# Transposing graph masks by DMA instead of on TensorE, and computing symmetric attention scores from their upper blocks only

## The chip, the cores and the metric

The kernel runs on one core of a Trainium2 chip. The metric is the device time of one execution in microseconds (us). A core has a matrix engine (TensorE; PE in the profile, with its weight loads as PEld), VectorE (DVE), ScalarE (ACT), GpSimd (POOL) and SyncE (SP), which here only issues DMA transfers. All work in parallel, each through its own instructions in order, and wait for each other by semaphores.

## The reference

Thirty-two graphs of 512 nodes with 256 features pass through four layers. Every layer normalises `x`, applies a ReLU, runs a graph layer and adds the result to `x`. The masks come from `adj`, which has an entry for each pair of nodes.

```
for each graph (x is 512 x 256, adj is 512 x 512, integers):
  layer 0: 4 heads; e = leaky_relu(src_i + dst_j), masked by adj > 0, softmax over j, times Wh, ELU
  layer 1: e = leaky_relu(s1_i + s2_j), masked by adj > 0, softmax over i, times h W, ELU
  layer 2: e = leaky_relu( sum_d h[i,d] a_k[d] h[j,d] ), a_k picked by adj == k+1
           alpha = softmax over j; out = alpha h
  layer 3: transformer block of 8 heads, mask adj | adj^T | eye, feed-forward 256 -> 1024 -> 256, two layer norms
  x = x + layer(relu(layernorm(x)))       (no change of shape between layers)
```

In the inputs `adj` holds only 0 and 1 and is symmetric with a full diagonal. In layer 2 then only `a_0` is used, and the raw score `e` is symmetric in i and j by its formula, whatever the inputs.

## The kernel before

**What a graph's work is.** A graph's rows are cut into `NT = 4` tiles of 128. `masks` makes `m = max(adj, 0)` in bf16 (tag `e0`), its transpose `mT` (tag `mT`, three buffers) and `m3`, the union of both with the diagonal, for layer 3. It transposes by TensorE: for each block column j, four 128x128 transposes with `ident_b` into one PSUM tile `ps_m`, then a VectorE copy into `mT[:, j]`. `layer0` to `layer3` follow. Most matmuls have f32 operands, and each of those appears in the profile as two passes with a weight load each; transposes of f32 data (`ps_t`) take one.

**Layer 0 around the masks.** The factors of the softmax are worked out per row (`rt`), transposed (`ps_sp`), copied (`spr`), written to DRAM (`rows0_d`) and read back spread over all partitions (`rows0`, 1 MB). Each of 16 products `p0` is one VectorE operation on `rows0`, `rt` and `mT[:, j]`. So the first `p0` needs `rows0` and a `mT`. The products feed the matmuls into `ps_o`.

**Layer 2 before.** With `h2T` the transposed features and `ha` the same scaled by `a_0`, each block row j of the scores is one PSUM tile `ps_e` of 128x512, from two f32 matmuls over the two halves of the features. ScalarE takes two exponentials of it (`y1`, `y2`), VectorE their maximum and its product with `mT[:, j]`, which is `p[:, j]`. Then `ps_o2` takes four matmuls for each row tile, over the four `p[:, j]`.

**What sets the order.** Nothing is emitted directly. Every operation is recorded as a job of a `Plan`, on one engine, in the order of the code. A table of whole numbers, `PLACES`, gives each job of a graph its place; graph b's jobs lie `b * ROUND` later, and places of one graph span about five `ROUND`s, so that up to five or six graphs are in work at once. `carry_out` sorts all jobs by place and chains those of each engine in that order:

```python
j.place = (self.number * ROUND + self.table[self.at], self.at)
```

The costs that the code gives beside each operation (as the `0.7` of `plan.matmuls(0.7, ...)`) are the planner's and have no effect when the kernel is built. All DMAs of the graphs are issued by SP in this one order (`plan.dma`, line 229). All DVE, ACT and POOL operations carry the helper's line 208 in the profile, matmuls 242 and transposes 240.

`Kind` gives buffers in turn. PSUM tags `ps_a` and `ps_b` have two slots each; `ps_m`, `ps_t`, `ps_e`, `ps_sp` and others all take turns in `ps_a`.

Of the kernel before, what the change touches and what calls it, by code (L numbers as in the profile page):

```python
# [12 lines left out]
BF = mybir.dt.bfloat16  # L13
I32 = mybir.dt.int32
U8 = mybir.dt.uint8
AF = mybir.ActivationFunctionType
# [3 lines left out]
P = 128  # L20
EPS = 1e-5
SLOPE = 0.2
# [100 lines left out]
class Plan:  # L123
# [5 lines left out]
        tensor_mul=(1, 2), tensor_add=(1, 2), tensor_max=(1, 2), scalar_tensor_tensor=(1, 3),  # L129
# [120 lines left out]
def cut(i, n):  # L250
    return slice(i * n, (i + 1) * n)
# [6 lines left out]
def width(args):  # L258
# [4 lines left out]

ROUND = 100000
PLACES = [
    101057, 0, 123766, 132584, 138431, 138431, 129046, 129834, 141740, 143105, 134508, 134509, 144040, 210061,
    161002, 171169, 182168, 133665, 13191, 13021, 30954, 43154, 22726, 43431, 38536, 68458, 82755, 86554,
    111786, 130752, 129745, 131659, 123328, 131022, 131022, 131659, 131659, 132269, 131903, 131903, 133024,
    133024, 133652, 134925, 134925, 135696, 134926, 135221, 136062, 136062, 136599, 136118, 136118, 137150,
    137150, 137545, 137150, 137150, 139783, 140391, 142870, 141719, 141719, 143128, 143129, 144853, 148260,  # L270
    148260, 152426, 148876, 155076, 157818, 157819, 157819, 157819, 164437, 164708, 163596, 155574, 152987,
    160713, 176876, 177710, 177710, 179541, 182264, 183463, 176075, 182822, 185309, 181512, 188918, 191812,
    194790, 194790, 195416, 200809, 186592, 166060, 200276, 196368, 206502, 219397, 219397, 220179, 220236,
    220236, 220993, 220993, 220993, 236727, 260248, 225731, 224396, 221012, 226847, 227931, 225205, 226679,
    229220, 229909, 230823, 231592, 233629, 234505, 234416, 235736, 236254, 236255, 236255, 236658, 236658,
    235736, 235736, 235736, 235737, 235737, 238980, 239538, 240610, 238111, 238111, 238138, 238912, 238912,
    239366, 238681, 238681, 238759, 245139, 243744, 247134, 245207, 246602, 251006, 252746, 255282, 256553,
    256553, 267976, 284322, 258231, 258231, 266098, 274931, 278417, 259592, 268181, 276573, 276814, 280405,
    258871, 269299, 271252, 271252, 276979, 286007, 286230, 286230, 286719, 286775, 284782, 285553, 285553,
    285554, 286042, 304459, 316500, 292215, 286775, 286775, 286712, 286042, 286947, 286999, 286712, 286042,  # L280
    289012, 290864, 292270, 295476, 295301, 295110, 300417, 301246, 301273, 301546, 301877, 303799, 304417,
    304978, 304978, 304978, 305067, 305193, 305509, 305551, 305551, 307045, 307452, 312018, 312812, 308660,
    308660, 308661, 309600, 309600, 318033, 314173, 314173, 314937, 314173, 314937, 319853, 320002, 320002,
    320288, 320059, 320288, 320288, 322248, 322248, 322403, 323086, 324116, 324117, 325432, 326217, 328750,
    326427, 329903, 331583, 335374, 344646, 332413, 334123, 331714, 333807, 334483, 334355, 336218, 333807,
    336218, 342666, 350313, 355600, 351966, 356396, 352228, 358089, 358678, 360971, 360971, 360971, 360971,
    363748, 363748, 364342, 369127, 379803, 380423, 380423, 382964, 384060, 384225, 371529, 374051, 378404,
    379308, 383266, 381312, 383855, 383855, 383855, 384091, 384645, 384645, 384645, 384645, 385299, 385400,
    385400, 385400, 385400, 389820, 388261, 386697, 387002, 387597, 387826, 400724, 398878, 392051, 393887,
    394199, 394199, 404354, 403089, 401043, 401043, 404073, 405950, 407212, 407456, 407456, 407584, 413067,  # L290
    415663, 415663, 420500, 420500, 420500, 405416, 406883, 405416, 406883, 409976, 409216, 407761, 407761,
    407761, 407761, 418999, 418111, 412219, 414095, 414095, 414095, 421851, 420227, 418886, 419104, 419104,
    419859, 422460, 421229, 422921, 429525, 422921, 422921, 422921, 428527, 429230, 429525, 356784, 429933,
    430027, 431151, 431151, 433611, 433611, 435044, 435044, 435798, 415663, 455098, 467528, 430623, 437997,
    437034, 435798, 436926, 438396, 438153, 438202, 438170, 438463, 438463, 439032, 439044, 439854, 439997,
    440219, 439866, 439866, 440054, 440689, 440689, 440689, 440690, 440690, 443133, 443701, 454267, 467213,
    448784, 448785, 448785, 448785, 448785, 450704, 444131, 444131, 445620, 445620, 445620, 445620, 445901,
    446700, 446700, 446700, 446701, 446701, 449901, 449901, 449901, 450807, 460195, 461219, 459629, 463106,
    463106, 463106, 463106, 463106, 463106, 463207, 464695, 464695, 464695, 464695, 464695, 464696, 464696,
    465450, 467213, 465756, 465756, 465756, 465756, 466107, 466107, 466108, 466561, 466561, 467895, 467931,  # L300
    467931, 467932, 467932, 467932, 467932, 471404, 467213, 468235, 473585, 474076, 467537, 472797, 474594,
    474655, 475293, 475293, 475293, 478979, 479362, 479362, 479362, 479362, 480230, 503393,
]


# [1 line left out]
def quick_path(  # L307
# [6 lines left out]
    B, N, D = x.shape  # L314
    NT = N // P
    KD = D // P
# [31 lines left out]
    def new(tag, name, shape, dtype=F32):  # L348
        return plan.tile(K[tag], name, shape, dtype)
# [133 lines left out]
    def masks(b, adj_t):  # L483


        m = new("e0", f"m_{b}", [P, NT, N], BF)
        plan.dve("tensor_scalar_max", m, adj_t, 0, each=0.52e-3)
        kinds = new("kinds", "kinds", [P, 1])
        plan.act("activation", adj_t, adj_t, AF.Relu, bias=none, accum_out=kinds, fixed=0.5)
        mT = new("mT", f"mT_{b}", [P, NT, N], BF)  # L490
        for j in range(NT):
            ps = new("ps_a", "ps_m", [P, NT, P], BF)
            plan.matmuls(0.7, *((ps[:, i], m[:, i, cut(j, P)], ident_b) for i in range(NT)))
            plan.dve("tensor_copy", mT[:, j], ps.shaped("p a b -> p (a b)"), each=0.52e-3)
        m3 = new("m3", f"m3_{b}", [P, NT, N], BF)
        plan.dve("tensor_max", m3, m, mT, each=0.52e-3)
        for i in range(NT):
            plan.dve("tensor_max", m3[:, i, cut(i, P)], m3[:, i, cut(i, P)], ident_b, each=0.52e-3)
        plan.dve("scalar_tensor_tensor", ok[:, 0:1], kinds, 0.0, ok[:, 0:1], OP.is_le, OP.mult)
        return mT, m3  # L500
# [100 lines left out]
    def layer2(b, x_t, mT):  # L601
        h = new("h1", f"h2_{b}", [P, NT, D + 1])
        plan.pool("memset", h[:, :, D], 1.0)
        normed(x_t, h, AF.Relu)
        hT = transposed_a(h, "h1T", f"h2T_{b}")
        ha = new("wh1", f"ha_{b}", [P, NT, D + 2])
        ha_k = [ha[:, 2 * k : 2 * k + 2, :D] for k in range(KD)]
        for k in range(KD):
            plan.dve(
                "tensor_scalar_mul", ha_k[k], hT[:, k].split("p (a b) -> p a b", (2, D), a=2), a2_t[:, k : k + 1],  # L610
                each=0.52e-3, fixed=0.2,
            )
        p = new("p1", f"p2_{b}", [P, NT, N])
        for j in range(NT):
            ps = new("ps_a", "ps_e", [P, N])
            for k in range(KD):
                plan.matmuls(FULL, (ps, ha_k[k][:, j // 2, cut(j % 2, P)], hT[:, k], k == 0, k == KD - 1))

            y1, y2 = (new("y", "y2", [P, N]) for _ in range(2))
            plan.act("activation", y1, ps, AF.Exp, bias=nshift, fixed=0.27)  # L620
            plan.act("activation", y2, ps, AF.Exp, bias=nshift, scale=SLOPE, fixed=0.27)
            plan.dve("tensor_max", y1, y1, y2)
            plan.dve("tensor_mul", p[:, j], y1, mT[:, j])
        inv = new("inv2", "inv2", [P, NT])
        for i in range(NT):
            ps = new("ps_a", "ps_o2", [P, N])
            plan.matmuls(
                NT * HALF,
                *((ps[:, : D + 1], p[:, j, cut(i, P)], h[:, j], j == 0, j == NT - 1) for j in range(NT)),
            )  # L630
            plan.dve("reciprocal", inv[:, i : i + 1], ps[:, D : D + 1], fixed=0.16)
            plan.dve(
                "scalar_tensor_tensor", x_t[:, i], ps[:, :D], inv[:, i : i + 1], x_t[:, i], OP.mult, OP.add, fixed=0.21
            )
        within(inv, NT)
# [630 lines left out]
```

## Time and profile before

| | |
|---|---|
| median of 10 runs | 3957.23 us (3953.45 to 3960.96) |
| profiled execution | 3958.52 us, span of the profile 3956.7 us |
| mean granted TensorE clock | 0.979 |
| PE busy | 3785.6 us, 96% of the span |
| PE weight loads | 2383.9 us, 60% |
| DVE busy | 2596.2 us, 66% |
| ACT busy | 1891.2 us, 48% |
| POOL busy | 781.0 us, 20% |
| from one graph's output transfer to the next, in the middle | 117.9 us |

"Busy" is the time in which at least one instruction of the engine is in work. Matmuls overlap: one with 512 columns is shown as 592 ns, but the next of its kind starts 429 ns after it. In a group of instructions the mean is that of one, and the idle time is that of the engine just before the instructions of the group. The window view gives the busy time of each engine in a stretch of the span.

### The profile page before, as it was taken

The page shows a single profiled execution, that of the slowest core. Times are in us where ns is not written, and L with a number is a line of the kernel's source. Part 1 is how long each engine was busy: PE and PEld are TensorE (multiplying, and loading weights), DVE is VectorE, ACT ScalarE, POOL GpSimd, SP SyncE. Part 2 cuts the span into 40 slices and gives each one's busy share as a digit, 9 for nine tenths or more (in the row PEclk, how much of TensorE's full clock was granted, in tenths as well). Part 3 has the DMA queues.
Part 4 walks back from the last instruction along what each step waited for, and adds up shares of the span by engine and source line. Part 5 has one row for each costly group of instructions (what it writes and reads, how often), then busy time and mean ns, then how long its engine had stood idle before and what let it go on. Part 6 is the DMA issues. An engine that isn't in the chain of part 4 may idle for free. (4 is left out here: it accounts for less than half of the span.)

```text
span 3956.7 us, 51981 instructions
## 1 busy us (share of the span) xinstructions
PE 3785.6 (96%) x20294; PEld 2383.9 (60%) x20294; DVE 2596.2 (66%) x5115; ACT 1891.2 (48%) x3297; POOL 781.0 (20%) x618
## 2 busy tenths in 40 slices
PE   5799999999999999999999999999999999999996
PEld 4556666656666556566656666656666655666543
DVE  4576666767666776666776666776766676766532
ACT  1255444555444554444555544555444455544442
POOL 0011222111222112222121222211122211222211
PEclk7799999999999999999999999999999999999998
DMA  3111110110110110110110110111111011110000
GB/s 99 48 34 33 38 44 23 44 44 28 41 41 23 44 44 28 41 41 23 44 44 28 42 40 28 38 44 34 37 38 43 24 44 40 32 34 27 17 12 13
DMA packets 99278, 144.62 MB, mean 37 GB/s; under 512 B 29008, under 2 KB 65360, under 8 KB 94928
## 3 DMA queue, kind: packets, MB, share of 16 engines
q1 hardware_dynamic: 92672, 136.22, 10.8%
q10 hardware_dynamic: 6352, 4.99, 0.4%
q8 instruction: 162, 2.65, 0.3%
q14 instruction: 92, 0.75, 0.1%
HBM read 122.96 MB, written 18.22 MB: 36 GB/s over the span
## 5 line engine op out<-in xcount | busy, mean ns | idle before, releaser
L242 PEld LDWEIGHTS ps_o<-wh,p 128*128 128x128 f32 x5120 | 706.8, 197 | 252.1 <-issue 183.8
L208 DVE TENSOR_TENSOR p<-p,m 128x2048 f32<-128x2048 f32 x256 | 582.3, 2285 | 332.0 <-ACT p L208 327.6
L242 PE MATMUL ps_o<-wh,p 128*128 128x65 f32 (+1 forms) x5120 | 762.1, 303 | 27.9 <-DVE p L208 27.9
L208 ACT ACTIVATE p<-ps_s 128x1024 f32<-128x1024 f32 x512 | 496.5, 1021 | 331.1 <-PE ps_s L242 255.8
L208 POOL TENSOR_SCALAR rstd<-mv 128x4 f32<-128x4 f32 x192 | 105.4, 549 | 2493.9 <-DVE mv L208 2201.6
L208 DVE SCALAR_TENSOR_TENSOR p<-rows,rt,mT 128x512 f32<-128x512 f32 x512 | 431.6, 865 | 250.1 <-PE ps_o L242 140.2
L242 PE MATMUL ps_f<-tT,ff_t 128*128 128x512 f32 x1024 | 455.8, 600 | 13.7 <-ACT tT L208 13.7
L242 PE MATMUL ps_f<-ff_t,f 128*128 128x256 f32 x2048 | 457.6, 379 | 0.0
L242 PEld LDWEIGHTS ps_f<-ff_t,f 128*128 128x128 f32 x2048 | 381.9, 190 | 48.5 <-issue 0.5
L208 ACT ACTIVATE h<-x,shift,rstd 128x256 f32<-128x256 f32 x512 | 275.1, 593 | 208.3 <-DVE shift L208 123.4
L242 PEld LDWEIGHTS ps_f<-tT,ff_t 128*128 128x128 f32 x1024 | 191.2, 192 | 248.7 <-issue 212.9
L242 PE MATMUL ps_s<-qk 32*128 32x512 f32 x2048 | 297.2, 642 | 0.3
L242 PE MATMUL ps_to<-p,ones 128*32 128x512 f32 x2048 | 267.8, 606 | 10.0 <-DVE p L208 10.0
L208 ACT ACTIVATE f<-ps_f,ff1b_c 128x512 f32<-128x512 f32 x256 | 161.3, 681 | 240.2 <-PE ps_f L242 240.2
L242 PE MATMUL ps_ct<-p,v 128*32 128x512 f32 x2048 | 272.2, 604 | 0.4 <-DVE p L208 0.4
L242 PE MATMUL ps_e<-h2T,ha 128*128 128x512 f32 x512 | 253.9, 618 | 2.5 <-ACT y L208 1.9
L242 PE MATMUL ps_o<-h,p 128*128 128x257 f32 x1024 | 239.7, 386 | 1.9 <-DVE mv L208 1.1
L242 PE MATMUL ps_qk<-h3T,wqkv_t 128*128 128x512 f32 x512 | 239.8, 602 | 1.1 <-ACT h3T L208 1.1
L242 PEld LDWEIGHTS ps_o<-h,p 128*128 128x128 f32 x1024 | 188.7, 189 | 79.7 <-issue 54.5
L208 DVE TENSOR_TENSOR u<-ps_f,n 128x512 f32<-128x512 f32 x64 | 44.3, 692 | 276.1 <-PE ps_f L242 276.1
L208 DVE BATCH_NORM_STATS2 st<-x 128x6 f32<-128x256 f32 x512 | 205.6, 414 | 8.2 <-DMA x<-in_x_dram 4.9
L208 POOL TENSOR_TENSOR rstd<-rstd,nhalf 128x4 f32<-128x4 f32 x192 | 208.3, 1089 | 13.4
(114 smaller groups left out, 4838.4 us busy)
## 6 DMA issues: line engine op xcount, KB each, us to landing
adj<-in_adj_dram SPq DMA_DIRECT2D x32, 1024.0 KB
rows<-rows_d SPq DMA_DIRECT2D x32, 1024.0 KB
x<-in_x_dram SPq DMA_DIRECT2D x32, 512.0 KB
rows<-rows_d SPq DMA_DIRECT2D x32, 512.0 KB
inv<-in_d SPq DMA_DIRECT2D x256, 64.0 KB
out_dram<-y SPq DMA_DIRECT2D x32, 512.0 KB
ff_t<-in_L_gnn_W_dram ACTq DMA_DIRECT2D x2, 1024.0 KB
to_d<-to SPq DMA_DIRECT2D x64, 8.0 KB
```

The costliest lines, as they stand in the source:

```text
L208: return [getattr(unit, method)(*map(real, args), **{k: real(v) for k, v in kw.items()})]
L242: made.append(self.nc.tensor.matmul(*map(real, c[:3]), start=c[3], stop=c[4]))
```

## The change

The masks are no longer transposed by TensorE. For each row tile i of `m` SP issues one DMA transpose, which moves the 128x512 bf16 tile into column block i of all four `mT[:, j]`. Every `mT[:, j]` is complete only when all four have landed.

In layer 2, of block row j only the column blocks from j on are worked out: `ps_e` has 512, 384, 256 and 128 columns, and so have the exponentials and the maximum. The blocks below the diagonal are had by transposing the blocks `y1[:, i]` with i > j on TensorE into a new PSUM tile `ps_y` (six 128x128 f32 transposes for each graph), and VectorE multiplies `ps_y` with the mask into `p`. `PLACES` is a new table as a whole, so that every engine's order changes.

```diff
 PLACES = [
-    101057, 0, 123766, 132584, 138431, 138431, 129046, 129834, 141740, 143105, 134508, 134509, 144040, 210061,
...
+    5095, 0, 75421, 87257, 75421, 75422, 79730, 91873, 132389, 236254, 196081, 207636, 243857, 181976, 44107,
...
         mT = new("mT", f"mT_{b}", [P, NT, N], BF)
-        for j in range(NT):
-            ps = new("ps_a", "ps_m", [P, NT, P], BF)
-            plan.matmuls(0.7, *((ps[:, i], m[:, i, cut(j, P)], ident_b) for i in range(NT)))
-            plan.dve("tensor_copy", mT[:, j], ps.shaped("p a b -> p (a b)"), each=0.52e-3)
+        for i in range(NT):
+            plan.dma(mT[:, :, cut(i, P)], m[:, i], 0.5, 1.2, "dma_start_transpose")
...
         p = new("p1", f"p2_{b}", [P, NT, N])
         for j in range(NT):
+            on = slice(j * P, N)
             ps = new("ps_a", "ps_e", [P, N])
             for k in range(KD):
-                plan.matmuls(FULL, (ps, ha_k[k][:, j // 2, cut(j % 2, P)], hT[:, k], k == 0, k == KD - 1))
+                plan.matmuls(
+                    FULL * (NT - j) / NT,
+                    (ps[:, on], ha_k[k][:, j // 2, cut(j % 2, P)], hT[:, k, on], k == 0, k == KD - 1),
+                )
 
             y1, y2 = (new("y", "y2", [P, N]) for _ in range(2))
-            plan.act("activation", y1, ps, AF.Exp, bias=nshift, fixed=0.27)
-            plan.act("activation", y2, ps, AF.Exp, bias=nshift, scale=SLOPE, fixed=0.27)
-            plan.dve("tensor_max", y1, y1, y2)
-            plan.dve("tensor_mul", p[:, j], y1, mT[:, j])
+            plan.act("activation", y1[:, on], ps[:, on], AF.Exp, bias=nshift, fixed=0.27)
+            plan.act("activation", y2[:, on], ps[:, on], AF.Exp, bias=nshift, scale=SLOPE, fixed=0.27)
+            plan.dve("tensor_max", y1[:, on], y1[:, on], y2[:, on])
+            if j < NT - 1:
+                ps = new("ps_a", "ps_y", [P, NT, P])
+                for i in range(j + 1, NT):
+                    plan.matmuls(0.11, (ps[:, i], y1[:, cut(i, P)], ident))
+                plan.dve("tensor_mul", p[:, j + 1 :, cut(j, P)], ps[:, j + 1 :], mT[:, j + 1 :, cut(j, P)])
+            plan.dve("tensor_mul", p[:, j, on], y1[:, on], mT[:, j, on])
```

In the order of SP, the first three transposes of a graph stand after the read of the layer 1 rows (`rows1`) of the graph two before. The fourth stands between the write of the same graph's `rows0_d` and the read of `rows0`, and the loads of the next graph follow.

## The prediction

> **What bounds the kernel now.** The first view is the page's table of 40 slices, the second the window view.
>
> ```profile
> PE   5799999999999999999999999999999999999996
> DVE  4576666767666776666776666776766676766532
> PEclk7799999999999999999999999999999999999998
> ```
>
> ```profile
> 0.00:200.00 200.00, 126.05 (x556) 103.44 (x557) 102.72 (x252) 46.48 (x105) 13.56 (x26) 0.74 0.23 73
> 200.00:3800.00 3600.00, 3543.72 (x19278) 2219.79 (x19277) 2459.10 (x4797) 1799.20 (x3126) 737.82 (x572) 1.00 0.11 36
> 3800.00:3956.00 156.00, 115.84 (x464) 60.63 (x462) 34.43 (x68) 45.54 (x66) 29.64 (x20) 0.84 0.04 11
> ```
>
> The columns after the length are PE, PEld, DVE, ACT and POOL busy, then granted clock, DMA share and GB/s. From 200 to 3800 us PE is busy 98.4% of the time at the full clock; DVE stands at 68%, ACT at 50%, the DMA engines at 11%. At 117.9 us between outputs this stretch is 30.5 of the 32 graphs, and only 56 us of it, 1.8 us for each graph, have no matmul. So PE's work sets the time, and what leaves PE comes off the time unless a new wait replaces it. The third view is the groups by form:
>
> ```profile
> L242 PE MATMUL ps_f<-ff_t,f 128*128 128x256 f32 x2048 | 457.6, 379 | 0.0
> L242 PE MATMUL ps_f<-tT,ff_t 128*128 128x512 f32 x1024 | 455.8, 600 | 13.7 <-ACT tT L208 13.7
> L242 PE MATMUL ps_e<-h2T,ha 128*128 128x512 f32 x512 | 253.9, 618 | 2.5 <-ACT y L208 1.9 <-DVE ha L208 0.5
> L240 PE MATMUL ps_t<-ident,h 128*128 128x128 f32 x1024 | 173.4, 284 | 13.4 <-ACT h L208 12.0 <-DVE mT L208 0.7 <-DVE inv L208 0.6
> L240 PE MATMUL ps_m<-ident_b,m 128*128 128x128 bf16 x512 | 50.2, 221 | 9.9 <-DVE m L208 6.1 <-DVE h0T L208 1.1 <-DVE bo_r L410 0.5
> ```
>
> Since matmuls overlap, the price of one is not its mean but busy time over count: 0.445 us for a pass of 512 columns (455.8/1024), 0.223 for 256 (457.6/2048), 0.169 for a 128x128 f32 transpose (173.4/1024, ends of short groups included).
>
> **The change, part by part, all 32 graphs together.**
>
> *Mask transposes leave PE.* The `ps_m` group is 50.2 us busy and 9.9 idle: a gain of 50 to 60 us; I take 55.
>
> *Fewer score columns.* Each graph had 16 passes of 512. It will have four each of 512, 384, 256 and 128. At 0.445, 0.334 (between its neighbours), 0.223 and 0.14 (between half of 0.223 and 0.169) that is 4 x 1.142 = 4.57 us against 16 x 0.445 = 7.12, a gain of 2.55 us for each graph, 82 us in all. Taking 6/16 off the group's own 253.9 us gives 95. I take 85, since the passes of `ps_e` stand in pairs and their ends are in the group's figure.
>
> *Six f32 transposes for each graph come to PE.* 192 x 0.169 = 32 us, which I take; 192 x 0.11 = 21 if they follow each other closely, 192 x 0.284 = 55 if each stands alone. The built order has them as three and three single ones.
>
> PE in sum: -55 - 85 + 32 = -108 us, bounds -78 (50 + 82 - 54) and -134 (60 + 95 - 21). In 91% of the span (3600 of 3957 us) PE is full; in the rest chains and loads bound it, and I count half: -108 x 0.955 = -103.
>
> *The other engines get lighter.* DVE loses 128 mask copies (53.1 us) and 6/16 of the columns of the maximum and of the product (87.4 and 85.4 us busy; less than 6/16 off, since a short operation has a fixed part). It gains three products from PSUM of 384, 256 and 128 columns; near rows are 0.42 us for 256 (`o<-ps_o,rt`) and 0.69 for 512, so about 1.25 us for each graph. Net near -2 us of 81 a graph. ACT drops by about 1.5 us a graph. Neither is the bound, so both count nothing by themselves.
>
> *The transposes on SP.* This is the unknown: the trace shows no DMA transpose. What it shows is SP's normal work and how soon the rows come back:
>
> ```profile
> 2058.53 0.30 SPq L229 DMA_DIRECT2D rows_d<-spr  x1
> 2059.86 0.34 SPq L229 DMA_DIRECT2D rows<-rows_d  x1
> ...
> 2064.80 1.41 DVE L208 SCALAR_TENSOR_TENSOR p<-rows,rt,mT 128x512 f32<-128x512 f32 x2 [3.45 <-DMA rows<-rows_d]
> ```
>
> An issue takes SP 0.3 us; `rows0_d` has landed 1.33 us after its issue began, and `p0` starts 4.8 us (here 4.9) after the read's issue. Say that each transpose holds SP, and the transfers behind it, for x us. The lowest x is 0.3, the row above. A high one: 128x512 bf16 values in runs of one 128-row column (256 bytes) are 512 packets; the page's q1 row has 92672 packets in 10.8% of 16 engines' 3957 us, 74 ns each, so 512 x 74 / 16 = 2.4 us. Packets of single elements would be far worse, 128 times that, and nothing in the trace excludes them. I take 1.4, in the middle of 0.3 and 2.4, because the transfer has plain whole rows at its source like the ordinary ones.
>
> What covers x? In the built order, between `m` and the fourth transpose PE has 32 passes of `ps_o` in layer 1 at 0.215 (6.9 us), 16 of `ps_wh` at 0.223 (3.6), two of `ps_qk` and four of `ps_v` (1.7), and three `ps_s`, two `ps_to` and two `ps_ct` groups at about 0.95 (6.7): 18.9 us. From `spr` to the first `p0` stand two `ps_s`, two `ps_to` and two `ps_ct` groups (5.8), eight `ps_t` (0.9) and `ps_e` of 512 and 384 columns (3.0): 9.7 us. `m` itself takes 1.2 us. So rows0's read is issued the later of 1.33 and 0.3 + x us after `rows0_d`'s issue, and the `p0` is due at 18.9 + 9.7 = 28.6 us after `m` begins. For x over 1.0 it can start at max(18.9, 1.2 + 3x) + 0.3 + x + 4.8. At x = 1.4 that is 25.4: 3.2 us early. Nothing is late for x up to 4.6 us. Queued behind a transpose on SP are only rows0's write and read, then the next graph's `x` and `adj` (used half a round later) and an output, which nobody waits for. The waits for `to_d`, `part`, `in_d` and `inv` come over 10 us of matmuls later. So I cost SP's part at nothing.
>
> Here a rule of the skill speaks against the change. The Trainium skill, "VectorE: DVE Perf Modes", section "The three transpose paths", gives 390 ns for a 128x128 bf16 transpose on TensorE and 1309 ns for one by DMA, and advises TensorE where PSUM will do. The `ps_m` row shows 98 ns each on TensorE (50.2/512), so the page's TensorE price is not this kernel's. By the page's DMA price, an estimate, x would be 4 x 1.309 = 5.2 us, and `p0` 0.6 us late: some 19 us of the gain gone, not all.
>
> *The new chain in layer 2.* `ps_e` to two exponentials (0.68 each), maximum (0.68 or less), `ps_y`, product, `ps_o2`. It needs 2.1 us and hops before `ps_y`. The built order has 5 to 6 us of other matmuls between each `ps_e` and its transposes (`ps_s`, `ps_ct`, `ps_to` groups), so it is covered; PSUM loses four holders of `ps_a` a graph and gains three. I cost it at nothing; without the cover it is 2 us for each of three block rows.
>
> *Waits on PE that may go.* Of PE's idle time 27.9 us are waits of `ps_o` for a DVE `p`, in the same stage where DVE now waits 3.4 us a graph for `rows0` (the waits view, 109.8 us in all). The new order puts 9.7 us between `spr` and `p0`, so this DVE wait should go. I count a third of the 27.9, -10, between 0 and -28, and +15 for unknown new waits on the other side.
>
> The profiled execution took 3958.5 us, 1.8 more than its span and 1.3 more than the median. 3958.5 - 103 - 10 - 1.3 = 3844 us. The forecast's own range is 3805 to 3890: the PE bounds, with waits from -20 to +15.
>
> **Rivals.**
>
> *Slow transposes: slower than before.* If x is above 4.6 us, `p0` comes late, DVE stands with the layer 3 products `p3` queued behind it, and soon PE waits for `ps_to` and `ps_ct`. By the formula it is even with before where the delay equals the 3.4 us a graph that PE gains, at x = 6.4. At x = 8 `p0` starts at 25.2 + 13.1 = 38.3, 9.7 late: 6.3 net a graph, times 31 is 195, so 4152 us. For it: no row prices a DMA transpose. Against: the DMA engines are only 11% busy, and 256-byte packets give 2.4. A delay at `p0` is here taken as fully PE's.
>
> *The gain is partly given back.* The table is new as a whole, so other waits of PE can open, above all in layer 2: half of its 6 us cover missing would cost 1 us for each of three block rows, 3 x 31 = 93 us, and leave 3937, at worst no change. For it: `ps_y` sits on a chain over three engines. Against: the distances in the built order.
>
> *The work isn't saved.* Symmetric scores need the lower blocks too; if the order still had 16 full passes nothing would be gained. The built order shows the short ones, so this has no chance of its own.
>
> **How the numbers follow.** My forecast has 0.72, the given-back gain 0.13 (3890 to 3948), slow transposes 0.12, and 0.03 is left for no change. A measurement can tell 0.2% of this kernel, 8 us. Faster: 0.72 + 0.13 = 0.85; same 0.03; slower 0.12. The range takes in my own and the greater part of the second case: 3790 to 3935.
>
> **What would show it.** Right: outputs 114 to 115 us apart; no `ps_m` group; 512 `ps_e` passes with together 150 to 170 us busy; 192 `ps_y`; SP's transposes each 0.3 to 2.4 us, with the fourth of a graph delaying `rows` by under 2 us; no long DVE wait for `rows`. Wrong: transposes over 4.6 us, DVE waiting for `mT` or `rows` with PE idle before `ps_o` or `ps_to`; or PE idle before `ps_y` or `ps_o` of layer 2 for more than 1 us a graph.

## The result, and the profile after

The change made the kernel slower: 3976.24 us (median, 3970.73 to 3982.79) against 3956.47, a ratio of 1.005 with an interval of 1.0041 to 1.0059. The forecast was 3844 us, range 3790 to 3935. The profiled execution has a span of 3968.4 us and a mean granted clock of 0.978.

The window view of after, with the columns of before:

```profile
0.00:200.00 200.00, 125.61 (x551) 104.38 (x552) 96.84 (x239) 41.30 (x99) 8.53 (x23) 0.76 0.28 83
200.00:3800.00 3600.00, 3503.62 (x18926) 2174.67 (x18926) 2413.22 (x4766) 1740.79 (x3132) 733.23 (x575) 1.00 0.14 40
3800.00:3968.00 168.00, 121.85 (x501) 65.84 (x499) 40.96 (x78) 45.94 (x67) 29.75 (x20) 0.84 0.05 14
```

In the middle TensorE is busy 3503.6 of 3600 us, where it was 3543.7. So work did leave it, and the idle time grew from 56 to 96 us. Outputs follow each other by 118 us on average, as before. The groups by form show that the planned work is there:

```profile
L242 PE MATMUL ps_e<-h2T,ha 128*128 128x512 f32 x128 | 63.4, 618 | 1.0 <-DVE m L208 1.0
L242 PE MATMUL ps_e<-h2T,ha 128*128 128x384 f32 x128 | 58.0, 536 | 0.0
L240 PE MATMUL ps_y<-ident,y 128*128 128x128 f32 x192 | 49.0, 310 | 0.8 <-DVE y L208 0.8
L242 PE MATMUL ps_e<-h2T,ha 128*128 128x256 f32 x128 | 36.2, 405 | 1.6 <-DVE p L208 1.6
L242 PE MATMUL ps_e<-h2T,ha 128*128 128x128 f32 x128 | 19.6, 276 | 0.0
```

The `ps_e` passes are busy 177.2 us in sum where they were 253.9 (the prediction's sign of being right was 150 to 170), `ps_m` is gone, and `ps_y` waits for nothing (0.8 us in all). The transposes on SP are as cheap as assumed. This line of the view of the tile `mT` has least, median and longest time in ns:

```profile
L229 SPq DMA_TRANSPOSE mT<-m x128: 1188/1251/2372, 16.7 to 3553.3; - x128
```

What TensorE waits for shows the difference. The waits view, first of before and then of after, each over 20 periods from 1000 us on (total, number, longest):

```profile
PE ps_wh L242 <- ACT rt L208: 10.0, 20, 0.5
PE ps_f L242 <- ACT tT L208: 7.7, 20, 0.4
PE ps_wo L242 <- DVE cT L208: 5.6, 19, 0.4
PE ps_t L240 <- ACT h L208: 4.6, 20, 0.2
PE ps_sp L240 <- ACT rt L208: 3.5, 20, 0.2
```

```profile
PE ps_f L242 <- DVE o L208: 25.0, 20, 1.3
PE ps_t L240 <- ACT h L208: 21.8, 60, 0.8
PE ps_wo L242 <- DVE cT L208: 5.4, 5, 1.4
PE ps_t L240 <- DVE h1T L208: 2.0, 3, 0.8
```

Most of the old small waits are gone, and two new ones take their place: 1.25 us a graph for VectorE's `o` and 1.1 us for ScalarE's `h`. Neither is in layer 2 or at the masks. The timeline of after shows where the second comes from (start, length, engine):

```profile
2108.43 2.35 POOL L208 TENSOR_TENSOR x<-x,b_r 128x1024 f32<-128x1024 f32 x1
2108.49 2.30 DVE L208 SCALAR_TENSOR_TENSOR shift<-mv,rstd 128x4 f32<-128x4 f32 x1 [1.47 <-POOL rstd L208]
...
2110.83 0.60 ACT L208 ACTIVATE y<-u,shift,rstd 128x256 f32<-128x256 f32 x1 [2.19 <-DVE shift L208]
...
2111.34 2.06 ACT L208 ACTIVATE h<-x,shift,rstd 128x256 f32<-128x256 f32 x4
...
2111.98 0.82 PE L240 MATMUL ps_t<-ident,h 128*128 128x128 f32 x3 [0.76 <-ACT h L208]
```

`shift` is 4 columns wide and takes 2.30 us. It begins 0.06 us after a GpSimd operation of 1024 columns and ends with it; ScalarE's `y` and `h` and TensorE's `ps_t` stand behind it. The wait for `o` begins in the same way, 36 us earlier:

```profile
2072.47 2.35 POOL L208 TENSOR_TENSOR n<-n,g_r 128x1024 f32<-128x1024 f32 x1
2072.53 2.31 DVE L208 SCALAR_TENSOR_TENSOR shift<-mv,rstd 128x4 f32<-128x4 f32 x1 [1.47 <-POOL rstd L208]
...
2074.76 3.45 DVE L208 TENSOR_TENSOR mc<-rows,mT 128x512 f32<-128x512 f32 x2
...
2074.89 2.76 POOL L208 TENSOR_TENSOR n<-n,b_r 128x1024 f32<-128x1024 f32 x1
...
2079.72 0.42 DVE L208 TENSOR_TENSOR o<-ps_o,rt 128x256 f32<-128x256 f32 x1
...
2080.28 1.10 PE L242 MATMUL ps_f<-ff_t,f 128*128 128x256 f32 x4 [1.25 <-DVE o L208]
```

Here a blocked `shift` and then a blocked `mc` hold up VectorE's queue, in which `o` stands five operations later. The view of the tile `shift`, first of before, then of after:

```profile
L208 DVE SCALAR_TENSOR_TENSOR shift<-mv,rstd x192: 139/161/165, 15.1 to 3944.7; 128x4 f32<-128x4 f32 x192
```

```profile
L208 DVE SCALAR_TENSOR_TENSOR shift<-mv,rstd x192: 148/161/2312, 15.3 to 3956.4; 128x4 f32<-128x4 f32 x192
```

Of after's 192 `shift` 61 take over 1 us, of before's none. All 61 begin inside a GpSimd operation of 1024 columns, 32 times `x` and 29 times `n`. The Trainium skill, "SBUF — State Buffer", section "SBUF: two separate sides", says that VectorE and GpSimd share one pair of ports as an exclusive lock, held for a whole instruction, and that among others it concerns VectorE instructions with two tensors from SBUF, against GpSimd instructions that read SBUF. The rows agree so far: `shift` reads `mv` and `rstd` from SBUF, and it ends with the GpSimd operation of 2.35 us beside which it began. Whether the number of tensors decides it, only the runs below can show.

### The profile page after: what moved, and what is told of

It is laid out like the page before. It is cut to its first block, busy times and chain, and to the rows that moved or that the text cites. A ratio compares the mean times of both kernels' runs of the same rounds, so it can differ in the third digit from the quotient of the medians.

```text
span 3968.4 us, 51876 instructions
## 1 busy us (share of the span) xinstructions
PE 3751.1 (95%) x19974; PEld 2344.9 (59%) x19974; DVE 2551.0 (64%) x5083; ACT 1828.0 (46%) x3297; POOL 771.5 (19%) x618
## 5 line engine op out<-in xcount | busy, mean ns | idle before, releaser
L242 PE MATMUL ps_o<-wh,p 128*128 128x65 f32 (+1 forms) x5120 | 758.2, 302 | 23.1 <-DVE p L208 21.1
L208 ACT ACTIVATE p<-ps_s 128x1024 f32<-128x1024 f32 x512 | 506.1, 1023 | 214.2 <-PE ps_s L242 143.0
L208 POOL TENSOR_SCALAR rstd<-mv 128x4 f32<-128x4 f32 x192 | 47.5, 247 | 2272.4 <-DVE mv L208 2122.0
L242 PE MATMUL ps_f<-tT,ff_t 128*128 128x512 f32 x1024 | 482.1, 605 | 3.4 <-ACT tT L208 2.6
L208 DVE SCALAR_TENSOR_TENSOR p<-rows,rt,mT 128x512 f32<-128x512 f32 x512 | 367.4, 744 | 42.1 <-PE ps_o L242 28.2
L208 POOL TENSOR_TENSOR rstd<-rstd,nhalf 128x4 f32<-128x4 f32 x192 | 257.9, 1347 | 13.4
L240 PE MATMUL ps_t<-ident,h 128*128 128x128 f32 x1024 | 202.1, 292 | 57.7 <-ACT h L208 36.1
L240 PEld LDWEIGHTS ps_t<-ident,h 128*128 128x128 f32 x1024 | 126.0, 145 | 207.8 <-ACT h L208 110.7
L208 DVE SCALAR_TENSOR_TENSOR shift<-mv,rstd 128x4 f32<-128x4 f32 x192 | 161.1, 839 | 125.5 <-POOL rstd L208 125.5
```

The lines of the kernel that those rows point to most:

```text
L208: return [getattr(unit, method)(*map(real, args), **{k: real(v) for k, v in kw.items()})]
L240: made.append(self.nc.tensor.transpose(*map(real, c)))
L242: made.append(self.nc.tensor.matmul(*map(real, c[:3]), start=c[3], stop=c[4]))
```

## The experiments

Two questions stood against each other. Did the parts give what was forecast, and the new order of the instructions lost it? Or was TensorE's saved time worth nothing, because each wait grows by what is taken out ahead of it? The table `PLACES` can be kept or exchanged apart from the work, so each part was run in the old order, and the new order without its blocked `shift`. In the tables a ratio is to the kernel before on the same chip. Some expectations mark their theories with letters: A is that the parts give what was forecast and the order loses it, B that the DMA transposes disturb, C that layer 2's chain waits or short passes cost as much as long ones, D that the blocked `shift` holds up TensorE.

### The parts in the old order

The masks by transfers alone: before's table, the four transposes in the stead of the `ps_m` passes and their copies.

```diff
-        for j in range(NT):
-            ps = new("ps_a", "ps_m", [P, NT, P], BF)
-            plan.matmuls(0.7, *((ps[:, i], m[:, i, cut(j, P)], ident_b) for i in range(NT)))
-            plan.dve("tensor_copy", mT[:, j], ps.shaped("p a b -> p (a b)"), each=0.52e-3)
+        for i in range(NT):
+            plan.dma(mT[:, :, cut(i, P)], m[:, i], 0.5, 1.2, "dma_start_transpose")
...
-    138431, 138431, 129046, 129834, 141740, 143105, 134508, 134509,
+    129231, 129232, 129233, 129234,
```

> The kernel before with its own table of places and one part of the change: masks by four DMA transposes, at one place each just after the second inv3 transfer; layer 2 as before. Theory A (the new order as a whole is at fault, its operations save what was forecast): PE loses the ps_m groups, 1.4 to 1.9 us a graph, and the time is about 3956 - 45 = 3911 us (3895 to 3925). Theory B (the DMA transposes themselves disturb, by SP's 1.25 us each or by the DMA engines): 3950 us or more, with waits for mT or rows in the trace.

Layer 2's half in before's table, without and with the masks by transfers. The code is that of the change. The places of layer 2's scores stay as they were, and the `ps_y` transposes and their products got places behind the first three maxima. These are the places put in (for the first maximum three `ps_y` and a product, for the second two and a product, for the third one and a product):

```
triangle alone:   312585 x3, 313188; 319165 x2, 319174; 318925, 318925
with the masks:   312711 x3, 312711; 319289 x2, 319586; 321512, 322200
```

> The kernel before with its own table and only the other part: scores on and above the diagonal, the blocks below by ps_y transposes, put into the old order right behind the maximum they need; masks by TensorE. Theory A: PE loses about 2.5 and gains 1 us a graph, about 3956 - 45 = 3911 us (3895 to 3925). Theory C (the chain of layer 2 over three engines waits, or the short passes cost PE as much as the long ones): 3945 us or more, with PE idle before ps_y or ps_o of layer 2.

> Both parts of the change in the old order. Theory A: the sum of the two, about 3956 - 95 = 3861 us (3840 to 3890), so that the change itself is good and the new table loses it. Theories B or C: 3945 us or more. In between, some 3910, would say that half of the forecast gain is not there in any order.

| kernel | us | ratio |
|---|---|---|
| masks, old order | 3949.9 | 0.9988 (0.9979 to 0.9997) |
| triangle, old order | 4033.8 | 1.0187 (1.0173 to 1.0201) |
| both, old order | 4016.0 | 1.0148 (1.0133 to 1.0164) |

In the old order the masks were worth 5 us of the forecast's 55. TensorE's timeline says in part why; first of before, then of the masks alone, at the same place of the period:

```profile
2057.34 0.39 PE L240 MATMUL ps_m<-ident_b,m 128*128 128x128 bf16 x4
2057.91 0.28 PE L240 MATMUL ps_sp<-ident,rt 128*16 128x128 f32 x1 [0.17 <-ACT rt L208]
```

```profile
2055.24 0.28 PE L240 MATMUL ps_sp<-ident,rt 128*16 128x128 f32 x1 [0.46 <-ACT rt L208]
```

One of the four `ps_m` groups of a graph stood ahead of a wait. Without it TensorE reaches `ps_sp` sooner and waits 0.46 us instead of 0.17; over the period the waits grow by 0.4 us. The period falls by some 0.4 us (117.9 to 117.5), where `ps_m` took 1.4 us from start to start; the rest of the difference was not traced. A few longer periods, one of 121.0 us in which the granted clock fell, take back half of the gain.

With layer 2's half the old order becomes slower than before. The waits view of both parts in the old order:

```profile
PE ps_y L240 <- DVE y L208: 44.7, 32, 2.7
PE ps_e L242 <- DVE p L208: 20.2, 31, 0.7
```

The chain from `ps_e` over exponentials and maximum to `ps_y` isn't covered there: 1.4 us a graph before `ps_y`, and 0.65 us before the next `ps_e`, which waits for a product on VectorE, by the code the one that still reads a PSUM tile of the same tag. These waits use up most of the gain. That the time is even longer than before's is in part the granted clock. TensorE's timeline of both parts in the old order, and the window view of a stretch right behind its first lines:

```profile
1094.27 0.52 PE L240 MATMUL ps_y<-ident,y 128*128 128x128 f32 x3 [1.36 <-DVE y L208]
1095.44 1.71 PE L242 MATMUL ps_e<-h2T,ha 128*128 128x256 f32 x4 [0.65 <-DVE p L208]
1097.08 1.94 PE L242 MATMUL ps_to<-p,ones 128*32 128x512 f32 x8
```

```profile
1095.90:1099.20 3.30, 3.30 (x16) 0.90 (x18) 3.30 (x6) 0.84 (x2) 0.00 (x0) 0.50 0.00 0
```

Behind the two waits the clock is at half for 3.4 us, and the `ps_to` group takes 1.94 us where it takes 1.04 to 1.07 at the full clock. This happens in 20 of the first 26 periods. The others have a median of 118.5 us, only 0.6 above before; over the 26 periods this adds some 24 of the 61 us by which the run is slower, and with the triangle alone some 31 of 79. (These are estimates from the distances between outputs in the profiled executions.)

The places were my choice, and better ones may exist; what is shown is the price of the chain without cover, in waits and in clock. The new table has the cover, as its `ps_y` row above shows. So for the old order the answer to the second question is yes in large part; of the new one it says nothing yet.

### The new order without the blocked shift

The changed kernel with only this edit; `shift` has then one tensor from SBUF, and the scale comes through a pointer:

```diff
-        plan.dve("scalar_tensor_tensor", shift, mv[:, :, 0], -1.0, rstd, OP.mult, OP.mult)
+        for i in range(NT):
+            plan.dve("tensor_scalar", shift[:, i : i + 1], mv[:, i, 0:1], rstd[:, i : i + 1], -1.0, OP.mult, OP.mult)
```

> The changed kernel, its table unchanged, with shift worked out by four one-column operations that read one SBUF tensor and a per-partition scalar, in place of one operation that reads two SBUF tensors. In the changed kernel 61 of 192 shift operations take 2.3 us in place of 0.16, each exactly as long as a POOL operation that began with it. Theory D (this blocking holds up ScalarE's normalising and with it PE): shift is no longer long, the PE waits for ACT h in front of ps_t and most of the wait in front of ps_f go, some 1.5 us a graph: about 3976 - 45 = 3931 us (3915 to 3950). Rival (another wait ends there just as late, or the period is set elsewhere): 3965 to 3976.

It took 3914.57 us (3911.16 to 3917.53), ratio 0.9895 (0.988 to 0.9911): 62 us less than the changed kernel, though VectorE has more instructions. The control is the same edit in the kernel before:

> The kernel before with its order, and only `shift` written as four one-column tensor_scalar operations (one tensor input from SBUF, the scale from a pointer) in place of one scalar_tensor_tensor with two. The control for the run with the same edit in the changed kernel. In the trace of before none of the 192 `shift` operations takes over 1 us, so there is no blocked one to free; VectorE gets about 0.36 us more work at each of 192 places, beside TensorE. Theory of the shared port: 3950 to 3962 us, within 0.2% of the kernel before. Rival (the other form is simply better, or eases VectorE wherever it stands): 3890 to 3925 us, as in the changed kernel.

3959.99 us, ratio 1.001 (1.0001 to 1.0019). The edit is worth nothing by itself; it pays where the order puts GpSimd's large operations beside `shift`. The views of the changed kernel with the edit, the tile `shift` and the waits of TensorE over the whole span:

```profile
L208 DVE TENSOR_SCALAR shift<-mv,rstd x768: 196/204/216, 14.7 to 3901.3; 128x1 f32<-128x1 f32 x192
```

```profile
PE ps_f L242 <- DVE o L208: 33.3, 28, 1.5
...
PE ps_t L240 <- ACT h L208: 7.2, 6, 3.5
```

No `shift` is blocked, though 244 of the 768 begin inside a GpSimd operation of 1024 columns, and the wait for `h` falls from 36.1 us to 7.2. The wait for `o` stays: with `shift` out of the way, the two `mc` ahead of `o` collide instead (`mc` has a mean of 1509 ns here, 1183 in after, 703 in before).

### The wait for `o`

Two numbers of the table put `rt` and `o` of layer 0's third pair of heads ahead of layer 1's `mc`, `mc` and `p` on VectorE:

```diff
-    143295, 150203, 150647, 145729,
+    143295, 149900, 149901, 145729,
```

> The changed kernel with the one-input `shift` (3914.6 us) and two numbers of the order besides: the `rt` and `o` of layer 0's third pair of heads are put ahead of three operations of layer 1 (`mc`, `mc`, `p`) that stood ahead of them on VectorE. In the run with the one-input `shift` TensorE waits 33.3 us in 28 waits for that `o`, since the two `mc` ahead of it take 4.9 us together beside GpSimd's `n`. Theory of the shared port, with TensorE as what sets the time: the waits go and 20 to 33 us with them, 3882 to 3897 us. Rival (the period is held by a chain through VectorE, and the wait moves to the next reader of what is now later): 3905 to 3920 us.

> The changed kernel with its two-input `shift` left as it is, and only the two numbers of the order changed: `rt` and `o` of layer 0's third pair of heads ahead of `mc`, `mc`, `p` of layer 1 on VectorE. In the trace of after TensorE waits 35.0 us in 28 waits for this `o`. If the two waits (for `o`, and the ones that the blocked `shift` makes) are of separate places and add up: 3940 to 3955 us. Rival (freeing `o` helps only where `shift` is freed too, as the next chain holds the period): 3965 to 3980 us.

| changed kernel with | us | ratio |
|---|---|---|
| one-input `shift` and `o` first | 3880.94 (3868.31 to 3885.91) | 0.9805 (0.9791 to 0.9818) |
| `o` first alone | 3934.35 (3924.05 to 3946.1) | 0.9937 (0.9923 to 0.995) |

The two repairs are worth 62 and 42 us apart and 95 together: separate places that nearly add up. With `o` first alone the wait for `o` is gone from the view and that for `h` stays (37.8 us, 89 times).

### The other side of the lock

If the port is held for one instruction, short instructions on GpSimd must help as well as another `shift`. The changed kernel as it was, but each 128x1024 operation of GpSimd in four pieces, for example

```diff
-        plan.pool("tensor_mul", n, n, g1_r.unsqueeze(1).to_broadcast([P, NT, D]))
+        for i in range(NT):
+            plan.pool("tensor_mul", n[:, i], n[:, i], g1_r)
```

> The changed kernel with its two-input `shift` and its order, but each of GpSimd's six 128x1024 operations of a graph issued as four of 128x256 at the same place. Sum of the work on GpSimd is the same or a little more. If the port is held for one whole instruction of GpSimd, a blocked `shift` waits some 0.6 us (a quarter of 2.35) instead of 2.3, and TensorE's waits for `h` behind it go: 3910 to 3935 us. Rival (the port is shared by rate, or the following pieces go first): `shift` takes 2.3 us still, 3970 to 3985 us.

> The version with the one-input `shift` and `o` first (3880.9 us), and besides GpSimd's six 128x1024 operations of a graph in four pieces each. No wait on the port is left there that TensorE sees: its waits from 1000 to 3300 us add up to under 0.5 us a graph. Theory: within 0.3% of 3880.9 us. Rival (blocked VectorE operations still cost TensorE something that the list of waits does not show): 3850 to 3870 us.

> The kernel before with its order, and only GpSimd's six 128x1024 operations of a graph issued as four of 128x256 at the same place: the control for the run with the same edit in the changed kernel (3877.5 us against 3976.2). In the trace of before VectorE's operations are blocked too (`p<-rows,rt,mT` up to 2.85 us, `m<-m,ident_b` up to 2.37, `ok<-rt,ok` up to 2.37), but no wait of TensorE in the middle of the span names them. Theory (the blocked operations cost time only where TensorE waits behind them, and here it does not): 3945 to 3965 us. Rival (pieces of GpSimd ease this kernel in any order): 3870 to 3930 us.

| kernel | us | ratio |
|---|---|---|
| changed kernel, GpSimd in pieces | 3877.52 (3872.22 to 3886.96) | 0.9798 (0.9785 to 0.9812) |
| one-input `shift`, `o` first, and pieces | 3880.59 (3876.61 to 3887.45) | 0.981 (0.9797 to 0.9824) |
| before, GpSimd in pieces | 3953.84 (3950.87 to 3957.26) | 0.9994 (0.9985 to 1.0003) |

The pieces alone take 99 us off the changed kernel, more than the 41 to 66 expected: `mc` is freed too (its mean is 839 ns, 1183 in after), and with it the wait for `o` is gone. They add nothing where both waits are gone already, and nothing in before. The timeline and the tile `shift` of the changed kernel in pieces:

```profile
2026.93 3.07 POOL L208 TENSOR_TENSOR n<-n,g_r 128x256 f32<-128x256 f32 x3
2026.99 0.68 DVE L208 SCALAR_TENSOR_TENSOR shift<-mv,rstd 128x4 f32<-128x4 f32 x1 [1.47 <-POOL rstd L208]
2027.60 1.81 DVE L208 TENSOR_TENSOR mc<-rows,mT 128x512 f32<-128x512 f32 x2
```

```profile
L208 DVE SCALAR_TENSOR_TENSOR shift<-mv,rstd x192: 152/161/695, 14.6 to 3874.0; 128x4 f32<-128x4 f32 x192
```

The two-input `shift` now waits for one piece of 0.73 us, and then VectorE and GpSimd take turns, instruction by instruction. An operation with one tensor from PSUM and one from SBUF isn't held up there: 29 of the 128 `o` begin inside a piece, and none takes over 0.43 us. GpSimd gets slower by it (941 us busy instead of 771), which nobody waits for.

### What the parts are worth in the new order

Two runs put work back into the changed kernel with the one-input `shift` (3914.57 us): all 512 columns in each `ps_e` pass, and the masks by TensorE again, with four pairs of places in the stead of the transposes' (the first experiment's edit reversed; the places are again my choice).

```diff
-                    FULL * (NT - j) / NT,
-                    (ps[:, on], ha_k[k][:, j // 2, cut(j % 2, P)], hT[:, k, on], k == 0, k == KD - 1),
+                    FULL,
+                    (ps, ha_k[k][:, j // 2, cut(j % 2, P)], hT[:, k], k == 0, k == KD - 1),
```

```diff
-    75421, 75422, 79730, 91873,
+    96090, 96590, 101754, 103754, 76777, 78777, 84923, 85923,
```

> The changed kernel with the one-input `shift` (3914.6 us), but layer 2's score passes write all 512 columns again; exponentials, maxima, products and the transposes of `y` stay as in the changed kernel. Only TensorE's work grows: start to start the ps_e passes take 7.42 us a graph in before and 5.19 us after, so 2.23 us a graph, 71 us in 32. If TensorE sets the time in the new order: 3970 to 3995 us. Rival (a chain that does not pass through these passes holds the period, as the waits of the runs in the old order show): 3915 to 3940 us.

> The changed kernel with the one-input `shift` (3914.6 us), but the masks are transposed by TensorE and copied by VectorE as in before, four groups of four passes and four copies put into the new order between the place of `m` and that of layer 0's first products with the mask. TensorE's work grows by 1.40 us a graph (the ps_m groups start to start in before), 45 us in 32, and VectorE's by four copies. If TensorE sets the time in the new order: 3950 to 3980 us, more if the places found are poor. Rival (as in the old order, where the masks by transfers gave only 5 us): 3915 to 3930 us.

Full columns: 3993.7 us (3984.06 to 3996.4), 79 us more. Masks by TensorE: 3941.26 us (3933.76 to 3952.85), 27 us more. In the new order work on TensorE is paid for, the columns in full (79 us for an expected 71) and the masks by more than half (27 for 45). That is the answer to the first question: the parts give, and the two blocked places of the order that came with them lost it. The new order with both parts taken out was not run.

## Why the prediction was wrong, point by point

**What bounds the kernel** was read rightly, and so was the direction of each part: with the port's two waits away the changed kernel runs at 3878 to 3881 us, inside the range.

**The step that failed** is the term for waits that open. The prediction says of VectorE and ScalarE "Neither is the bound, so both count nothing by themselves", and allows "+15 for unknown new waits". The two waits behind blocked VectorE instructions cost 95 to 99 us. The prediction did weigh that "other waits of PE can open", but looked for them "above all in layer 2", and bounded that rival at "at worst no change". The waits came where no work was changed, and none of its signs of a wrong step (long transposes, waits for `rows`, waits before `ps_y`) shows. The built order had held them: in after's trace GpSimd's `n` and `x` follow right on `rstd` 60 times, in the place where `shift` starts; in before's no operation of 1024 columns does. Two things were not asked of it: which VectorE instructions read two tensors from SBUF, and what GpSimd starts beside them. Before had such collisions too (`p<-rows,rt,mT` up to 2.85 us, `m<-m,ident_b` up to 2.37), but in the middle of the span no wait of TensorE names them.

**The sum for TensorE** was too large by a quarter. Start to start and per graph, over 20 periods: `ps_m` took 1.40 us (45 us in 32 graphs, taken at 55); the `ps_e` passes fell from 7.42 to 5.19 us (71 us, taken at 85). One reason is that a pass of 384 columns takes 415 to 427 ns instead of 334; in this order such passes stand in twos between groups of other tilings. `ps_y` takes 1.07 us (34 us, taken at 32). That is 82 us for 108, within the bounds. The waits of `ps_o` fell by 7 us (27.9 to 21.1), taken at 10. One slip: from the bounds of the sum and waits of -20 to +15 the forecast's own range comes to 3809 to 3898, not 3805 to 3890.

**From 3844 to 3881.** 25 us of the 37 are that sum (26 x 0.955). Some 9 are the clock, an estimate: in the run with one-input `shift` and `o` first, outputs are some 114.0 us apart in the middle, but 118.2 and 118.7 in the two periods in which the clock fell, 4.2 + 4.7 more. Each fall follows a wait of TensorE, of 1.23 and 1.37 us. The last 3 us stay open. The window view of that run:

```profile
1720.00:1840.00 120.00, 119.97 (x654) 75.91 (x652) 85.00 (x180) 60.77 (x110) 28.24 (x21) 1.00 0.16 44
1840.00:1960.00 120.00, 118.74 (x635) 75.89 (x632) 84.13 (x180) 58.39 (x105) 24.14 (x19) 0.97 0.14 41
...
2080.00:2200.00 120.00, 118.60 (x638) 75.34 (x634) 84.17 (x177) 58.37 (x105) 25.48 (x20) 0.97 0.14 41
```

**The transposes on SP** were right: x is 1.25 us (taken as 1.4), and the DVE waits for `rows` fell from 109.8 to 19.9 us. The Trainium skill, "VectorE: DVE Perf Modes", section "The three transpose paths", gives 1309 ns for one 128x128 block by DMA. By that price the prediction's estimate was 5.2 us for a transfer of four blocks; here such a transfer holds SP for 1.25 us, and when its blocks land the trace doesn't show.

**The chain of layer 2** was right for the built order, and without cover, in the old order, TensorE's waits before `ps_y` and `ps_e` come to 2.0 us a graph (44.7 and 20.2 us in 32), not to 2 us for each of three block rows; that the clock also fell behind such waits was foreseen nowhere.

**The first output** comes 23 us later (371.4 for 348.1 us), which looked like a loss at first; but 1416 matmuls precede it instead of 1331, 20 us more busy time, so that is work brought forward.

## What to carry to other kernels

When a change comes with a new order, read the whole new order and not only the changed stage: for each VectorE instruction with two tensors in SBUF, see which GpSimd instruction can start just before it, and which engine waits behind it. Where such pairs meet on a path, cut GpSimd's instructions into pieces, or give VectorE a form with one tensor; where they don't meet, both changed the time by 0.1% at most here. And a pass taken off a full engine is worth its time only if it doesn't stand just ahead of a wait of that engine. And where the saved work leaves waits of TensorE close together, look at the granted clock behind them too.

## What the runs showed of the hardware

- The lock is by instruction and takes no account of size: a 128x4 operation of 0.16 us took 2.3 us beside one of 2.35 us and at most 0.70 us beside pieces; the one-input form, begun 244 times beside one of 1024 columns, never took over 0.22 us.
- One stop of TensorE costs about 0.16 us more than the idle time that the profile shows: in the run with the one-input `shift`, a wait of 1.19 us before `ps_f` lengthened the distance between starts by 1.35 us, since the pass ahead of it is drawn 592 ns long and the next one otherwise starts 429 ns after it.
- The granted clock was 1.00 in every 120 us stretch from 400 to 3520 us in before and in after. In the profiled executions of the other kernels together it falls to half 53 times between 400 and 3500 us, for 3.4 to 10.2 us each, 14 and 20 times in the two old-order runs with layer 2's half. Each time TensorE had idled 0.85 to 2.27 us in the 3.4 us before. In before no 3.4 us hold more than 0.74 us of idle time; in after they hold up to 1.37 without a fall, so the idle time alone doesn't decide it. A high load doesn't bring the falls: they are most frequent where TensorE is busy some 116 of 120 us (both parts in the old order), and stretches of 119.97 of 120 us have none. That the stops cause them is not tested.
- One DMA transpose of 128x512 bf16 from SBUF to SBUF held SP for 1.19 to 2.37 us, median 1.25.
